# Factorization layer in float32: five wide trees of seven, squared-weight sums on ScalarE's accumulator, one queue for the first loads

## Chip, cores and metric

One core of one Trainium2 chip runs the whole kernel. The metric is the device time of one execution in microseconds; shown are the median and the extremes of three runs. Engine names in the profile: PE is TensorE, PEld its weight loads, DVE is VectorE, ACT is ScalarE, POOL is GpSimd, SP is SyncE (which here only issues loads and stores).

## What is computed

```python
def _L0_rec_ref(x, weight, lin_w, lin_b):      # x (1024, 512), weight (64, 512, 512), lin_w (512, 512)
    out_lin = x @ lin_w.T + lin_b
    xv = jnp.einsum('bf,efm->bem', x, weight)
    zp = jnp.einsum('bf,efm->bem', jnp.square(x), jnp.square(weight))
    interaction = 0.5 * jnp.sum(jnp.square(xv) - zp, axis=1)
    return out_lin + interaction
```

All is float32. The large part is `xv`: 1024 x 512 times 512 x (64 x 512). Its squares are summed over e (64 values). The term `zp` needs no large product: summed over e it is x² times the sum over e of weight², so the kernel builds that sum (512 x 512, tile `w2_sum`) and multiplies once, at the end.

## The kernel before, in words

**Tiling.** The output columns m come in groups: two of 16 and twenty of 24 columns. With e innermost a group of 24 has 24 x 64 = 1536 columns of weight, split into two halves (quadrants `w11`, `w12`, `w21`, `w22` by half of f and half of m; a quadrant is 2 chunks of 128 rows of f, 768 columns each).

**Outer level.** Each group is multiplied by a fast 2 x 2 x 2 scheme of seven products (Winograd's form of Strassen's), products 1 to 7 in the order 1, 6, 5, 2, 7, 4, 3. Their right operands are the four quadrants and the sums `T1`, `T2`, `w12` += `w22`, `w21` += `T2`, which DMAs with accumulation form (issued by POOL). Their left operands are seven sums of x, tiles `X1` to `X7`, prepared once at the start.

**Inner level.** Each outer product is again a fast scheme, a "tree". `tree` is the thin one: 7 products, two row blocks each, right operand 384 columns wide. `wide_tree` is a scheme of 20 products with 256 columns each; it is used for the outer products in `HK` and only in the groups of 24. The sums of weight columns that a tree needs are made on POOL into the ring `t`. Intermediate sums live in PSUM: banks `b1` and `b3` and the pairs `b2_0`, `b2_1` (the profile leaves the numbers out: `b`, with `_l` and `_r` for the two banks of a pair). ACT copies PSUM parts from bank to bank or to SBUF (`p5`, `p53`, shown as `p`), DVE adds finished parts to the targets `oa`, `ob`, `oc`, `od`. For an outer product in `EARLY`, the first parts are added to the earlier target at once on DVE, without a copy kept in `p`. `finish` squares a target (ACT) and sums it over e (DVE, `TENSOR_REDUCE acc<-...`).

**Squared weight.** `w_squares` squares each chunk of a quadrant on ACT into a scratch tile `wsq` and reduces it over e on DVE into `w2_sum`.

**Order.** The program is written as a list of operations with reads, writes and estimated costs. `Plan.order` simulates the engines and puts the operations of each engine into a fixed order by due times; the table `AHEAD_OF` shifts single due times. Additions whose operands are all in SBUF may go to DVE or POOL, whichever comes first in that simulation; those that read PSUM go to DVE. A wait is a semaphore wait in front of an instruction, and every engine works its list in order.

**Start and end.** First x and `lin_w` are loaded and the linear part is multiplied by the same outer scheme (`outer_products`), while the X tiles are prepared. At the end the same function multiplies x² with `w2_sum`, and the parts are joined and stored.

Of the kernel before, what the change touches and what calls it, by code (L numbers as in the profile page):

```python
# [16 lines left out]
P = 128  # L17
SEG = 128
ORDER = (1, 6, 5, 2, 7, 4, 3)
HK = (1, 5, 2, 7)  # L20
EARLY = (2, 7)
# [17 lines left out]
P53S = 2  # L39
AHEAD_OF = """  # L40
0:t6x 1:t29 2:2qu 3:2w 4:3gd7 5:2mat 6:-i 7:t4v 8:1kwd 9:1xp9 a:v6a b:xxr c:-4 d:3jg2 e:-r f:-j g:-r h:-2g
i:-g j:4x k:t l:-8 m:-2k n:1x o:4i6 p:2c q:9 r:-1w s:n t:-11 u:-1 v:-o w:17 x:1n y:1z z:k 10:-23 11:g 12:-16
13:4 14:24 15:r 16:-5 17:z 18:j 19:-k 1a:13 1b:-18 1c:e 1d:-2z 1e:4 1f:21 1h:17 1i:-f 1j:-k 1k:-1 1l:1m 1m:-5
1n:-26 1o:-o 1p:q 1q:-b 1r:1p 1s:-22 1t:9 1u:-10 1v:-5 1w:8 1x:-9 1y:i 1z:1u 20:1e 21:-10 22:o 23:-n 24:-2x
25:2 26:-2t 27:-1z 28:2c 29:1b 2a:1z 2b:-b 2c:22 2d:-23 2e:1p 2f:4 2g:-2y 2h:-j 2i:1h 2j:o 2k:9 2l:k 2m:-c
2n:1i 2o:-1z 2p:-2 2q:47 2r:2n 2s:-6 2t:c 2u:-20 2v:10 2w:-2 2x:-m 2y:-10 2z:i 30:4p 31:5c 32:1j 33:9 34:2x
35:n 36:-6 37:-2c 38:d 39:1e 3a:-n 3b:r 3c:1t 3d:j 3e:m 3f:2k 3g:-2s 3h:1v 3i:31 3j:-12 3k:-m 3l:-2f 3m:7b
3n:2 3o:1co 3p:-i 3q:e 3r:-1h 3s:1nz 3t:-1l 3u:3 3v:118 3w:17 3x:-x 3y:-1t 3z:n 40:r 41:4 42:-v 43:18 44:2pm
45:1j 46:-l 47:-t 48:-1c 49:l3 4a:b 4b:2g 4c:e 4d:36 4e:y 4f:1v 4g:16 4h:-q 4i:b 4j:1 4l:-1r 4m:-3c 4n:n 4o:z
4p:-f 4q:-1d 4r:13 4s:5 4t:y 4u:2g 4v:4 4w:1i 4x:1c 4y:-20 4z:1z 50:l 51:-12 52:-20 53:27 54:-z 55:9 56:-2s  # L50
57:1o5 58:g 59:-1j 5a:-2r 5b:2k 5c:i 5d:21 5e:-12 5f:-1q 5g:1ju 5h:2d 5i:25 5j:p 5k:-1l 5l:-k 5m:-1y 5n:3b
5o:h 5p:-3r 5q:20 5r:-28 5s:-b 5t:2a 5u:29 5v:-n 5w:-2b 5x:w1 5y:3 5z:-1e 60:22 61:-1u 62:24i 63:-1u 64:-33
65:5m 66:-r 67:3q 68:-13 69:11 6a:22 6b:p 6c:s 6d:-y 6e:e 6f:25 6g:k 6h:-o 6i:-1n 6j:1c 6k:-u 6l:u 6m:e8
6n:-2f 6o:-1j 6p:z 6q:1m 6r:23 6s:-x 6t:h 6u:-15 6v:-29 6w:-y 6x:15 6y:-6j 6z:19 70:-n 71:-1n 72:-7 73:1u
74:-1n 75:-2c 76:-1e 77:3p 78:1q 79:7 7a:-2 7b:-u 7c:16 7d:-t 7e:-13 7f:-13 7g:-m 7h:u 7i:-1 7j:1c 7k:2b 7l:1p
7n:r 7o:-d 7p:b 7q:-w 7r:-3a 7s:u 7t:-20 7u:-v 7v:2c 7w:-32 7x:-8c 7y:1a 7z:-5 80:2i 81:-e 82:-2a 83:-2j
84:-29 85:-27 86:-j 87:d 88:-16 89:-2v 8a:-1g 8b:-c 8c:fk 8d:-c 8e:-g 8f:-2d 8g:-k 8h:i 8i:1i 8j:z 8k:-5
8l:-1a 8m:-dh 8n:-a 8o:-d1 8p:a 8q:-k 8r:-f 8s:s 8t:28 8u:q 8v:-19 8w:-1b 8x:3n 8y:-26 8z:fo 90:2s 91:-24 92:b
93:a2 94:-6 95:1h 96:1f 97:2q 98:-2u 99:-39 9a:-1j 9b:-m 9c:-2e 9d:28 9e:-s 9f:yw 9g:-l 9h:-16 9i:-w 9j:a
9k:ln 9l:-j 9m:1 9n:n 9o:1s 9p:-17 9q:r 9r:2p 9s:7 9t:-i 9u:m 9v:41 9w:3h 9x:-2c 9y:-s 9z:-17 a0:7 a1:-t a2:j  # L60
a3:-1x a4:1p a5:5 a6:-a a7:2k a8:-2g a9:14 aa:-u ab:-r ac:-14 ad:7 ae:-r af:-1a ag:-1w ah:-d ai:1vp aj:1a
ak:14 al:-1n am:-v an:w ao:-1b ap:1s aq:u ar:z as:11 at:-11 au:1q av:15 aw:j ax:-1b ay:-2i az:1d b0:-38 b1:-3t
# [12 lines left out]
h1:h h2:27 h4:-1z h5:-2 h6:-h h7:-g h8:-2w h9:-24 ha:1n hb:1c hc:-j hd:3v he:-g hf:-s hg:-1u hh:-3i hi:-n
hj:1a hk:-n hl:-3x hm:-2k hn:-n ho:-24 hp:-31 hq:9 hr:66 hs:-13 ht:4 hu:3t hv:et hw:1c hx:33 hy:33 hz:95
i0:-3c i1:8 i2:1a i3:-t i4:d4 i5:h1 i6:2o i7:-1f i8:-18 i9:i ia:2s ib:-k ic:11 id:-1j ie:-g if:3 ig:-4 ih:q
ii:39 ij:-14 ik:17 il:-2a im:o in:-2z io:29 ip:-1r iq:-11 ir:c is:10 it:-35 iu:-p iv:-1k iw:r ix:-1i iy:-i1
iz:w j0:a j1:b9 j2:-14 j3:1m j4:5d j5:-t j6:-1u j7:-hg j8:-7y j9:-2p ja:2t jb:-ma jc:-69 jd:-qk je:29 jf:-b
jg:3c jh:-2x ji:-4f jj:-9f jk:-2c jl:4d jm:1k jn:-1r jo:-25 jp:li jq:-1z jr:-d jt:4g ju:5o jv:6a jw:-1k jx:3h  # L80
jy:x jz:1q k0:-v k1:-2 k2:z k3:-5k k4:-1z k5:-1l k6:1g k7:8 k8:2g k9:15 ka:-38 kb:-35 kc:-y kd:-u ke:x kf:1u
kg:36 kh:-13 ki:3k kj:3d kk:-c kl:-5b km:vc kn:kz ko:-o kp:11 kq:21z kr:-1a ks:-1c kt:4o ku:ay kv:1p kw:-a3
kx:-y ky:-1d kz:1gq l0:-14 l1:-4h l2:-1a l3:-4 l4:-f l5:2x l6:v l7:-1h l8:t l9:lj la:18x lb:m5 lc:3l ld:-1a
le:-1p lf:4 lg:-2u lh:xt li:20 lj:134 lk:ph ll:-c lm:-1d ln:-1 lo:11 lp:-2n lq:-l lr:di ls:l lt:-p lu:3 lv:14
lw:-19 lx:2i ly:23 lz:-i m0:26 m1:-1h m2:e m3:1l m4:-2w m5:-38 m6:-2 m7:2q m8:-15 m9:-18 ma:-q mb:-1e mc:-11
md:-1v me:-5 mf:19 mg:1y mh:x mi:i mj:-13 mk:28 ml:-ou mm:1f mn:4h mo:-e mp:-9 mq:-q mr:10 ms:-1x mt:e mv:-r
# [263 lines left out]
def kernel(  # L350
# [162 lines left out]
    def lw_in(q, c):  # L513
        o = lw(q, c)
        dma(o.ap, lw_src[:, ts(q * 2 + c, KH * C)], (), o.atoms, 0.65, 2.2, nc.scalar, 0.25)
# [647 lines left out]
```

## Time and profile before

| | |
|---|---|
| median of 3 runs | 1412.26 us (1411.76 to 1416.25) |
| the profiled execution: its own time, its span | 1414.87 us, 1413.1 us |
| mean granted TensorE clock | 0.994 |
| TensorE busy | 1388.7 us, 98% of the span |
| VectorE, ScalarE, GpSimd busy | 1179.7, 825.7, 1173.6 us |
| DMA moved | 251.85 MB, mean 178 GB/s |

The span runs from the first to the last instruction of the profiled execution. A row of the timeline gives the start, the time from the first start to the last end, the instruction, its count and in brackets the idle time of the engine ahead of it with what ended it. A row of the groups gives count, busy time and mean duration in ns of one, then the idle time ahead. A row of the stretches gives the stretch and its length, then busy time and count for PE, PEld, DVE, ACT and POOL, the granted clock, the DMA's busy share and GB/s. A row of the waits gives the total, how often and the longest, in us. A row of the loads gives the count, the KB of one and the median us from issue to landing.

### The profile page before, as it was taken

Reading aid. Unit: us, or ns where it says so; the run is one execution under the profiler, and the core shown is the slowest. Engines: PE = TensorE matmul, PEld = TensorE weight load, DVE = VectorE, ACT = ScalarE, POOL = GpSimd, SP = SyncE. Lnnn points to the kernel's source line nnn. Section 1 sums busy time; section 2 is a strip of 40 time slices with the busy share of each in tenths; the row PEclk is TensorE's granted clock in tenths of the full one; section 3 lists DMA queues with packets and bytes.
Section 4 is the critical chain, followed back from the end, with each engine's and each line's share of the span. In section 5 each row is a group of like instructions: output and inputs, shape, how many; then the busy total and the mean of one; then the engine's idle time right before and its main releaser. Section 6 shows DMA issues by size and latency. Waiting matters only on the chain.

```text
span 1413.1 us, 17921 instructions
## 1 busy us (share of the span) xinstructions
PE 1388.7 (98%) x5500; PEld 1034.9 (73%) x5500; DVE 1179.7 (83%) x1769; ACT 825.7 (58%) x1345; POOL 1173.6 (83%) x1118
## 2 busy tenths in 40 slices
PE   7999999999999999999999999999999999999998
PEld 5878767677776767777776777777677777767666
DVE  5577788888988888888888888888888888898876
ACT  3355555757566565756656565666656565665752
POOL 5999978888788878878887887888788798888884
PEclk8999999999999999999999999999999999999999
DMA  8588595867859596775959577595957759594775
GB/s 248 150 191 195 111 254 126 221 164 178 202 122 243 122 232 154 184 195 127 242 115 247 144 179 199 134 236 116 254 136 183 194 145 228 117 257 117 162 171 131
DMA packets 94943, 251.85 MB, mean 178 GB/s; under 512 B 30464, under 2 KB 33536, under 8 KB 94848
## 3 DMA queue, kind: packets, MB, share of 16 engines
q0 software_dynamic: 27712, 136.23, 49.3%
q1 hardware_dynamic: 66560, 113.43, 23.6%
q10 hardware_dynamic: 576, 1.05, 0.2%
q8 instruction: 45, 0.74, 0.2%
q14 instruction: 50, 0.41, 0.1%
HBM read 127.04 MB, written 6.19 MB: 94 GB/s over the span
## 4 chain that ended last, share of the span: by engine, by line
PE 91%; DMA 4%; POOL 3%; issue 1%; DVE 1%; ACT 0%; SPq 0%; POOLq 0%; ACTq 0%
PE b L490 40%; PE b_r L490 24%; PE b_l L490 24%; POOL t L446 2%; PE b_l L543 2%; PE b_r L543 1%; DMA T<-T1b 1%; DMA oc<-od 1%; DMA T<-T1a 1%; DMA oa<-xT 1%; POOL ob L482 0%; DMA T1a<-weight 0%; DMA w22a<-weight 0%; POOL X L446 0%; DVE oa L446 0%
## 5 line engine op out<-in xcount | busy, mean ns | idle before, releaser
L490 PE MATMUL b<-t,X 128*128 128x384 f32 (+1 forms) x1184 | 401.9, 471 | 3.8 <-DVE ob L446 2.1
L446 POOL TENSOR_TENSOR t<-t,w 128x512 f32<-128x512 f32 (+1 forms) x300 | 293.9, 998 | 36.0 <-PE b L490 25.2
L490 PEld LDWEIGHTS b<-t,X 128*128 128x128 f32 x1184 | 219.2, 190 | 131.2 <-DVE ob L446 10.1
L490 PE MATMUL b_l<-t,X 128*128 128x256 f32 x960 | 243.4, 380 | 0.0
L490 PE MATMUL b_r<-t,X 128*128 128x256 f32 x800 | 214.8, 380 | 0.2 <-POOL t L446 0.2
L490 PEld LDWEIGHTS b_l<-t,X 128*128 128x128 f32 x960 | 180.7, 190 | 34.1 <-ACT b_l L456 2.5
L446 POOL TENSOR_TENSOR t<-w 128x768 f32<-128x768 f32 (+1 forms) x88 | 160.2, 1824 | 33.2 <-DMA w<-T 21.2
L490 PEld LDWEIGHTS b_r<-t,X 128*128 128x128 f32 x800 | 150.3, 190 | 46.0 <-issue 2.8
L463 ACT ACTIVATE oa<-oa 128x768 f32<-128x768 f32 (+1 forms) x176 | 142.7, 823 | 58.6 <-DVE oa L446 47.7
L473 DVE TENSOR_REDUCE acc<-oa 128x12 f32<-128x768 f32 (+1 forms) x176 | 159.2, 921 | 6.8 <-ACT oa L463 6.6
L473 DVE TENSOR_REDUCE w_sum<-wsq 128x12 f32<-128x768 f32 (+1 forms) x176 | 159.1, 919 | 1.4 <-ACT wsq L463 1.2
L490 PE MATMUL b_r<-w,X 128*128 128x256 f32 x600 | 149.7, 380 | 0.5 <-issue 0.5
L490 PEld LDWEIGHTS b_r<-w,X 128*128 128x128 f32 x600 | 112.8, 190 | 20.2 <-ACT b_r L455 1.9
L463 ACT ACTIVATE wsq<-w 128x768 f32<-128x768 f32 (+1 forms) x132 | 107.0, 819 | 32.6 <-DMA w<-weight 22.1
L490 PE MATMUL b_l<-w,X 128*128 128x256 f32 x480 | 117.5, 381 | 0.9 <-ACT b_l L456 0.9
L490 PE MATMUL b<-w,X 128*128 128x384 f32 (+1 forms) x336 | 110.2, 456 | 2.1 <-DMA w<-T 2.1
L456 ACT COPY b<-b 128x768 f32<-128x768 f32 (+1 forms) x74 | 55.4, 748 | 92.0 <-PE b L490 56.8
L490 PEld LDWEIGHTS b_l<-w,X 128*128 128x128 f32 x480 | 90.3, 190 | 17.1 <-ACT b_l L456 4.7
L463 ACT ACTIVATE ob<-ob 128x768 f32<-128x768 f32 (+1 forms) x88 | 72.0, 822 | 47.4 <-DVE ob L446 45.3
L490 PE MATMUL b<-T,X 128*128 128x384 f32 (+1 forms) x264 | 90.3, 477 | 2.2 <-DMA T<-T1a 1.4
L490 PEld LDWEIGHTS b<-w,X 128*128 128x128 f32 x336 | 63.5, 190 | 30.7 <-DMA w<-T 2.5
L473 DVE TENSOR_REDUCE acc<-oc 128x12 f32<-128x768 f32 (+1 forms) x88 | 79.8, 920 | 5.0 <-ACT oc L463 4.8
(179 smaller groups left out, 2620.1 us busy)
## 6 DMA issues: line engine op xcount, KB each, us to landing
w<-weight SPq DMA_DIRECT2D x120, 384.0 KB, 6.9
ob<-od POOLq DMA_DIRECT2D x40, 768.0 KB, 11.4
oc<-od POOLq DMA_DIRECT2D x40, 768.0 KB, 12.9
T<-weight SPq DMA_DIRECT2D x40, 384.0 KB, 5.8
w<-T POOLq DMA_DIRECT2D x20, 768.0 KB, 5.8
T1a<-weight SPq DMA_DIRECT2D x20, 384.0 KB, 3.3
T1a<-weight POOLq DMA_DIRECT2D x10, 768.0 KB, 8.4
w22a<-weight SPq DMA_DIRECT2D x20, 384.0 KB, 10.9
```

Source lines behind the costliest of these rows:

```text
L446: return f(o.ap, a.ap, b.ap)
L456: return nc.scalar.copy(o.ap, i.ap)
L463: lambda _: nc.scalar.activation(o.ap, i.ap, AF.Square, scale=scale),
L473: nc.vector.tensor_reduce(o, x, axis=AX.X, op=ALU.add)
L490: nc.tensor.matmul(a.ap, b.ap, w.ap, start=start, stop=True, skip_group_check=True)
L543: nc.tensor.matmul(a.ap, b.ap, w(k).ap, start=first and k == 0 and j % 2 == 0, stop=True, skip_group_check=True)
```

## The change

Outer product 6 joins `HK`, so that five of seven trees are wide in the groups of 24. Products 3, 4 and 6 join `EARLY`. `w_squares` no longer reduces on DVE: every run of 64 columns (one m, all e) is one ACT instruction that squares into a scratch tile `unread` and writes the sum of its squares through ACT's accumulator into `w2_sum`; the `wsq` tiles go, and there are 2048 such instructions. The first loads of x and `lin_w` are ranked in one fixed order on SP (before, `lin_w` went through ACT's queue). The preparation sums of five X tiles are bound to DVE, one `p53` tile goes, a few costs of the planner are changed, and the table `AHEAD_OF` is another one throughout, so that the order on every engine changes.

```diff
-HK = (1, 5, 2, 7)
-EARLY = (2, 7)
+HK = (1, 5, 6, 2, 7)
+EARLY = (2, 3, 4, 6, 7)
-P53S = 2
+P53S = 1
+SUMMED = ('w11', 'w12', 'w21', 'w22')
+DIRECT = ()
+PREP = (6, 5, 2, 7, 4)
 AHEAD_OF = """
-0:t6x 1:t29 2:2qu 3:2w 4:3gd7 5:2mat 6:-i 7:t4v 8:1kwd 9:1xp9 a:v6a b:xxr c:-4 d:3jg2 e:-r f:-j g:-r h:-2g
...
-            o.latest = latest - ahead[o.sign]
+            o.latest = latest - ahead[o.sign] if o.rank is None else o.rank - 1e6
...
-    wsq_ring = ring([make(f"wsq{k}", WIDE) for k in range(2)])
+    wsq_ring = ring([make(f"wsq{k}", WIDE) for k in range(2 if len(SUMMED) < 4 else 0)])
+    unread = make("unread", E)
...
+    firsts = iter(range(100))
+
+    def first_load(o, i):
+        n = next(firsts)
+        dma(o.ap, i, (), o.atoms, 1.1 if n < 4 else 0.65, 2.2, 0.45, n)
+
     def lw_in(q, c):
-        o = lw(q, c)
-        dma(o.ap, lw_src[:, ts(q * 2 + c, KH * C)], (), o.atoms, 0.65, 2.2, nc.scalar, 0.25)
+        first_load(lw(q, c), lw_src[:, ts(q * 2 + c, KH * C)])
...
+    x_load(0, 0, 0)
     lw_in(0, 0)
-    x_load(0, 0)
+    x_load(0, 0, 1)
+    x_load(0, 1, 0)
     lw_in(1, 0)
-    x_load(0, 1)
+    x_load(0, 1, 1)
     lw_in(0, 1)
     lw_in(1, 1)
-    x_load(1, 1)
-    x_load(1, 0)
-    dma(bias.ap, lin_b.partition_broadcast(P), (), bias.atoms, 1.3, 2.2)
+    for h, q in ((1, 1), (1, 0)):
+        for k in range(KH):
+            x_load(h, q, k)
+    first_load(bias, lin_b.partition_broadcast(P))
...
-            tt(o, a, b, sub)
+            tt(o, a, b, sub, DVE if i in PREP else None)
...
         for k in range(KH):
-            i, sq = reg(w(g, q), k * mi * E, mi * E), reg(wsq_ring(), 0, mi * E)
-            square(sq, i)
+            i = reg(w(g, q), k * mi * E, mi * E)
             o = reg("w2_sum", (row * KH + k) * M + base[g] + col * mi, mi)
-            reduce(o.ap, sq, o.atoms)
+            if q not in SUMMED:
...
+            for m in range(0, mi, 4):
+
+                def emit(_, i=i, o=o, m=m):
+                    return [
+                        nc.scalar.activation(
+                            reg(unread).ap, Reg(i.tile, i.off + j * E, E).ap,
+                            AF.Square, accum_out=Reg(o.tile, o.off + j, 1).ap,
+                        )
+                        for j in range(m, m + 4)
+                    ][-1]
+
+                plan.add({ACT: 4 * 0.18}, emit, Reg(i.tile, i.off + m * E, 4 * E).atoms,
+                         Reg(o.tile, o.off + m, 4).atoms + reg(unread).atoms)
...
-        dma(four(r), lin_dram[:, c, ts(h, 4), :], (("lin", h, c),), r.atoms)
+        dma(four(r), lin_dram[:, c, ts(h, 4), :], (("lin", h, c),), r.atoms, 2.3)
...
-        dma_add(four(r, 0, cut), acc_dram[:, c, ts(h, 4), :cut], 4 * C,
+        dma_add(four(r, 0, cut), acc_dram[:, c, ts(h, 4), :cut], 5 * C,
```

How the order moves, at three places. In the rows a tile carries a number (`X_62` to `X_68` are X1 to X7, `w_69` is `w11`, `w_70` is `w12`, `w_71` is `w21`, `T_76` is `T2`), and what an instruction waits for stands in brackets: `Activation` is ACT's own signal, `DMAHW` and `DMASW` are loads.

First place: ACT in a group of the steady part, around the squares of `w12` and `w11` between the thin trees 4 and 3 and the next group's tree 1. Before:

```order
L463 ACTIVATE wsq_86<-w_70 128x768 [waits DMAHW4_49,DMASW3_49,DVE_49]
L463 ACTIVATE oa<-oa 128x2x384 [waits DVE_49] x2
L456 COPY p_1_83<-b 128x768 [waits PE_49]
L456 COPY b_1<-b 128x2x384 [waits PE_49]
L463 ACTIVATE oa<-oa 128x2x384 [waits Pool_49]
L463 ACTIVATE wsq_87<-w_70 128x768 [waits DMAHW5_49,DVE_49]
```

With the change, from one PSUM copy (`b_0<-b`) to the next (`b_1_l<-b_r`):

```order
L459 COPY b_0<-b 128x2x384 [waits PE_49]
L755 ACTIVATE unread,w_sum<-w_69 128x64 [waits Activation_49] x4
L466 ACTIVATE oa<-oa 128x2x384 [waits DVE_49]
L755 ACTIVATE unread,w_sum<-w_69 128x64 [waits DMAHW3_49,Activation_49]
L755 ACTIVATE unread,w_sum<-w_69 128x64 [waits Activation_49] x11
L755 ACTIVATE unread,w_sum<-w_71 128x64 [waits DMAHW3_49,DMASW5_49,Activation_49]
L755 ACTIVATE unread,w_sum<-w_71 128x64 [waits Activation_49] x3
L466 ACTIVATE oa<-oa 128x2x384 [waits DVE_49]
L466 ACTIVATE ob<-ob 128x2x384 [waits DMASW7_49,DVE_49]
L755 ACTIVATE unread,w_sum<-w_71 128x64 [waits Activation_49] x4
L459 COPY b_1_l<-b_r 128x512 [waits DVE_49,PE_49]
```

One square of a whole chunk, which waited for DVE to free a `wsq` tile, is now a run of single pieces, each of which waits for ACT's own signal; in all 32 pieces and 3 squares of `oa` and `ob` stand between these two copies (rows that repeat are left out above).

Second place: SP at the start. Before:

```order
L478 DMA oa<-xT 128x512 x2
L478 DMA ob<-xT 128x512 x2
L478 DMA oa<-xT 128x512 x4
L478 DMA od<-lin_b 128x512
L478 DMA w_69<-weight 128x512 x2
```

With the change:

```order
L481 DMA oa<-xT 128x512
L481 DMA ob<-lin_wT 128x512
L481 DMA oa<-xT 128x512 x2
L481 DMA ob<-lin_wT 128x512
L481 DMA oa<-xT 128x512
L481 DMA ob<-lin_wT 128x512 x2
L481 DMA ob<-xT 128x512 x2
L481 DMA oa<-xT 128x512 x2
L481 DMA od<-lin_b 128x512
L481 DMA w_69<-weight 128x512
```

All first loads stand on SP in the order in which the linear part uses them, ahead of the first weights.

Third place: PE in the thin trees 4 (`X_65`) and 3 (`X_64`) of a steady group. In tree 4 `b<-t` is product 5, in tree 3 too; product 3 writes to the same bank. Before:

```order
L490 MATMUL b<-t,X_65 128x384 x2
L490 MATMUL b_0_r<-t,X_68 128x256
L490 MATMUL b_1<-t,X_65 128x384 x2
L490 MATMUL b<-w_71,X_65 128x384 x4
L490 MATMUL b<-t,X_64 128x384 x2
L490 MATMUL b<-w22a,X_64 128x384 x4
```

With the change:

```order
L494 MATMUL b<-t,X_65 128x384 x2
L494 MATMUL b_0_r<-t,X_68 128x256
L494 MATMUL b_1<-t,X_65 128x384 x2
L494 MATMUL b<-w_71,X_65 128x384 x4
L494 MATMUL b<-t,X_64 128x384 x2
L494 MATMUL b<-w22a,X_64 128x384 x2
L494 MATMUL b_1<-t,X_65 128x384 x2
```

In tree 4 the same matmuls lie between products 5 and 3. In tree 3 the old order ran product 1 and product 3 right behind product 5, the new one has a product of tree 4 between them.

234 lines of the change are left out of this document (121 added, 113 removed).

## The prediction

> **What bounds the kernel now.** I read the page's busy times first, then the chain that ended last, then the busy times by stretch, then what TensorE waited for.
>
> ```profile
> PE 1388.7 (98%) x5500; PEld 1034.9 (73%) x5500; DVE 1179.7 (83%) x1769; ACT 825.7 (58%) x1345; POOL 1173.6 (83%) x1118
> PE 91%; DMA 4%; POOL 3%; issue 1%; DVE 1%; ACT 0%; SPq 0%; POOLq 0%; ACTq 0%
> 0.00:20.00 20.00, 10.80 (x26) 7.20 (x27) 6.50 (x8) 5.75 (x7) 8.07 (x12) 0.74 0.88 299
> 615.48:739.90 124.42, 124.20 (x490) 91.68 (x489) 107.81 (x162) 76.45 (x124) 104.33 (x97) 1.00 0.74 180
> PE b_l L543 <- DMA oa<-xT: 7.6, 1, 7.6
> ```
>
> TensorE is busy for 98% of the span and is 91% of the chain. The stretch 615.48 to 739.90 is two groups of 24 columns in the steady part: TensorE has work in 124.20 of 124.42 us, at a granted clock of 1.00. There the other engines have room: per group of 62.2 us, DVE works 53.9, ACT 38.2, POOL 52.2. Only the first 20 us show a long wait, 7.6 us for the first x. So the time is the sum of the matmuls; what shortens them counts in full as long as no other engine passes 61 us per group.
>
> **The change part by part.** *1. Tree 6 becomes wide in the 20 groups of 24 columns.* A thin tree is 7 products of 2 halves of 384 columns, a wide one is 20 products of 256; every float32 matmul stands in the trace as two instructions.
>
> ```profile
> 628.34 1.45 PE L490 MATMUL b<-t,X 128*128 128x384 f32 x4
> 629.63 1.45 PE L490 MATMUL b<-w22b,X 128*128 128x384 f32 x4
> 656.61 1.89 PE L490 MATMUL b_l<-T1a,X 128*128 128x256 f32 x8
> 658.33 1.89 PE L490 MATMUL b_r<-T1a,X 128*128 128x256 f32 x8
> ```
>
> From start to start, 4 instructions of 384 columns take 1.29 us (0.3225 each) and 8 of 256 take 1.72 (0.215 each). Thin: 28 x 0.3225 = 9.03. Wide: 40 x 0.215 = 8.60. That saves 0.43 per group, 20 x 0.43 = **8.6 us**. The same prices give 61.5 us for a group before (84 and 160 instructions) and 61.1 after (56 and 200); the 0.7 us between 61.5 and the measured 62.2 are small gaps that I leave as they are.
>
> *2. POOL and DVE.* POOL now makes tree 6's wide sums (one of 768, two of 512, four of 256) in place of one of 768 and two of 384. In return the wider EARLY set puts tree 6's, 3's and 4's first addend into the target straight from PSUM on DVE, so that three adds per group leave POOL.
>
> ```profile
> L446 POOL TENSOR_TENSOR t<-t,w 128x512 f32<-128x512 f32 x120 | 158.7, 1325 | 22.3 <-PE b L490 16.5 <-PE b_l L490 0.7
> L446 POOL TENSOR_TENSOR t<-t,w 128x256 f32<-128x256 f32 x180 | 135.6, 780 | 13.7 <-PE b L490 8.7
> L446 POOL TENSOR_TENSOR t<-T,t 128x384 f32<-128x384 f32 x40 | 40.0, 1001 | 3.1
> L446 POOL TENSOR_TENSOR ob<-p,ob 128x768 f32<-128x768 f32 x20 | 37.7, 1885 | 0.0
> L446 POOL TENSOR_TENSOR oa<-oa,oc 128x768 f32<-128x768 f32 x20 | 37.4, 1870 | 8.7 <-ACT oa L463 8.2 <-issue 0.5
> L446 POOL TENSOR_TENSOR ob<-ob,oa 128x768 f32<-128x768 f32 x20 | 36.3, 1816 | 3.8 <-ACT b_l L456 3.8
> L473 DVE TENSOR_REDUCE w_sum<-wsq 128x12 f32<-128x768 f32 x160 | 148.7, 944 | 0.5 <-ACT wsq L463 0.5
> L446 DVE TENSOR_TENSOR ob<-b,oa 128x768 f32<-128x768 f32 x60 | 57.3, 955 | 5.5 <-PE b L490 4.3 <-issue 0.5
> L446 DVE TENSOR_TENSOR oc<-ob,b_l 128x512 f32<-128x512 f32 x60 | 40.3, 683 | 3.4 <-ACT b_r L456 2.3 <-PE b_l L490 0.4
> L446 DVE TENSOR_TENSOR oc<-ob,b_r 128x256 f32<-128x256 f32 x120 | 46.6, 416 | 4.9 <-ACT p L456 3.8 <-PE b_r L490 0.3
> ```
>
> POOL per group: the 768 sum is in both; + 2 x 1.325 + 4 x 0.780 - 2 x 1.001 = +3.8, and three adds leave, -5.6: 50.4 of 61.1. DVE per group: eight reductions leave (148.7 / 20 = -7.4), three adds of 768 leave (-2.9), ten adds of 256 and five of 512 come (+4.2, +3.4): 51.2. Both get lighter, so neither costs time. One wait moves: in the thin trees 4 and 3 product 3 now overwrites the bank of product 5 after a DVE add (0.955) instead of an ACT copy (0.798, row below). The order of TensorE puts 1.7 us (tree 4) and 2.6 us (tree 3) of other matmuls between the two products; that covers it. Uncovered it would be 0.16 x 40 = 6 us.
>
> *3. ACT.* Off ACT: eight squares of 768, three copies p and one copy b of 768 per group. Onto it: tree 6's wide copies (four of 512, one of 256), and 96 squares of 64 columns per group whose sum goes out through the accumulator.
>
> ```profile
> L463 ACT ACTIVATE wsq<-w 128x768 f32<-128x768 f32 x120 | 99.6, 838 | 18.9 <-DMA w<-weight 16.8 <-DVE oa L446 1.3 <-DVE w_sum L473 0.2
> L456 ACT COPY p<-b 128x768 f32<-128x768 f32 x60 | 47.9, 798 | 22.4 <-PE b L490 21.1
> L456 ACT COPY b<-b 128x768 f32<-128x768 f32 x60 | 47.4, 790 | 80.7 <-PE b L490 46.1 <-DVE oc L446 32.4 <-PE b_r L490 1.0
> L455 ACT ACTIVATE b_r<-b_r 128x512 f32<-128x512 f32 x80 | 46.8, 585 | 30.0 <-DVE b_r L446 29.2
> L456 ACT COPY p<-b_r 128x256 f32<-128x256 f32 x120 | 44.8, 373 | 41.3 <-PE b_r L490 33.9 <-PE b_l L490 5.6 <-DVE oa L446 1.2
> L455 ACT ACTIVATE X<-X 128x128 f32<-128x128 f32 x4 | 1.2, 306 | 0.4 <-POOL X L446 0.4
> L456 ACT COPY t<-t 128x4 f32<-128x4 f32 x1 | 0.2, 195 | 0.0
> 706.65 0.59 ACT L455 ACTIVATE oa<-b_l 128x512 f32<-128x512 f32 x1
> 707.13 0.38 ACT L455 ACTIVATE oa<-b_r 128x256 f32<-128x256 f32 x1
> ```
>
> Without the pieces ACT has 38.2 - 8 x 0.83 - 3 x 0.80 - 0.79 + 4 x 0.58 + 0.37 = 31.1 us per group. The price c of a piece has no row. The rows of 128 and 768 columns differ by 0.83 ns a column, so a row of 64 lasts about 0.25. Independent instructions overlap: the row of 0.59 at 706.65 is followed after 0.48, so a free piece could start every 0.14 us. That is the lower end. But every piece writes the same scrap tile `unread`, and the order shows that each waits for ACT's own signal, so no piece begins before the last one has ended. What such a wait on the own engine costs, DVE shows:
>
> ```profile
> 583.62 0.94 DVE L473 TENSOR_REDUCE w_sum<-wsq 128x12 f32<-128x768 f32 x1
> 584.48 0.94 DVE L473 TENSOR_REDUCE acc<-oc 128x12 f32<-128x768 f32 x1
> 586.73 0.96 DVE L446 TENSOR_TENSOR ob<-b,oa 128x768 f32<-128x768 f32 x1
> 587.72 0.95 DVE L446 TENSOR_TENSOR ob<-ob,b 128x768 f32<-128x768 f32 x1
> ```
>
> A free instruction follows 0.08 before the end of the row ahead of it, the chained one (it adds to what was just written) 0.03 after. A chained piece is then 0.25 + 0.03 = 0.28 us if the sum costs nothing more, and if writing it out is a small step of its own (the copy of 4 columns, 0.195) 0.475: the upper end. I take 0.28, the row that a piece is most like. ACT has then 31.1 + 96 x 0.28 = 58.0 of 61.1 us, under TensorE but at 95%. ACT works in order, so a PSUM copy behind a run of pieces is late, and TensorE waits for copies (`b<-b`, `b_l<-b_l`): I charge 0.1 us per group, **+2 us**, between 0 and what rivals A and B give.
>
> The Trainium skill, ScalarE: Activation LUTs, section What ACT_TABLE_LOAD costs, gives an ACTIVATE with immediates 186 ns + 0.833 ns a column, with an overlap of about 93 ns between neighbours. For 64 columns this is 0.24 in a chain and 0.15 without; the 306 ns row is 13 ns above it, so the trace nearly agrees, and by 0.24 ACT would have 54 us per group.
>
> *4. First loads.* TensorE's first real matmul starts late:
>
> ```profile
> oa<-xT SPq DMA_DIRECT2D x6, 256.0 KB, 4.6
> L446 POOL TENSOR_TENSOR X<-X 128x256 f32<-128x256 f32 x48 | 43.2, 949 | 18.8 <-ACT X L456 6.0 <-DVE X L446 5.5 <-PE b_r L543 4.6
> 0.74 0.87 SPq L478 DMA_DIRECT2D oa<-xT  x2
> 5.21 1.04 ACT L456 COPY X<-oa 128x1024 f32<-128x1024 f32 x1 [2.98 <-DMA oa<-xT]
> 12.62 3.78 PE L543 MATMUL b_l<-ob,oa 128*128 128x256 f32 x8 [7.61 <-DMA oa<-xT]
> ```
>
> SP issues one load each 0.43 us; the first pair was issued by 1.61 and used by ACT at 5.21, 3.6 us later. Now the two loads of the first matmul, and the x behind them, are the first three on SP: issued by 2.04, landed about 5.7 instead of 12.6. The gain is at most 6.9 us. The loads behind them take 256 KB / 299 GB/s = 0.88 us each whatever their order, and the weights still come after all 13, so part is lost again where the first groups wait for DMA and POOL. Below it is 0. I take **5 us**: the operands of every later product of this stage land before TensorE gets to it. That tree preparation of five X moves from POOL to DVE takes 0.95 us each off a POOL that the first groups wait for; I count nothing for it.
>
> Sum: -8.6 - 5 + 2 = -11.6. It is made against the profiled execution (span 1413.1, its own time 1414.87, 2.6 above the median of 1412.26) and carried over to the median: **1401 us**.
>
> **The rivals.**
> A. ACT becomes the bound, slower. The place is the chain of pieces, the point a price of 0.324 us: then 31.1 + 96 c is the 62.2 us of a group before. If the written-out sum is an instruction of its own that overlaps by the 0.11 of the 706.65 row, c = 0.25 + 0.03 + 0.195 - 0.11 = 0.365 and a group takes 66.1: 1412 - 5 + 20 x 3.9 = 1485. At 0.475 it is 76.7, 1697. For it: the self-wait, and that no row shows a sum for free; against it: no row of ACT shows a separate step either. The Trainium skill, VectorE: DVE Perf Modes, section Two Vector instructions with no wait between them, says that an operation of VectorE that writes out its accumulator is two instructions; for ACT no run here shows it. This rule speaks for A.
> B. ACT stays below TensorE, but the runs are too long. In one group of the new order ACT has 32 pieces and 3 squares of `oa` and `ob` between two PSUM copies; at 0.28 these are 9.0 + 2.5 = 11.5 us, and 3 us less at a price of 0.19, the row of the smallest copy. If a third of these 3 us reaches TensorE, 1 us per group: 1401 - 2 + 20 = 1419. For it: 95% of ACT; against it: DVE at 87% of a group lets TensorE run now.
> C. The change of the loads does nothing. TensorE starts earlier and waits later, in the groups of 16, for DMA and POOL: 1406. For it: DMA is busy for 0.88 of the first 20 us.
>
> **How the numbers follow.** The forecast (1391 to 1407) has 0.42, C 0.14, B 0.14, A 0.30. A measurement of this kernel tells 0.3% (4 us) from no change. Faster takes the forecast and C, 0.56; B lies about the upper edge of no change, 0.08 there and 0.06 above it; with A slower has 0.36. The likeliest case's own range is 1391 to 1407. Half of A, where the written-out sum overlaps, lies under 1490; above that 0.15 and below 1391 some 0.03 are left out: 1391 to 1490.
>
> **What would show it.** Step 1: 200 matmul instructions of 256 columns per group instead of 160, 56 of 384 instead of 84, and a pair of groups at 123 to 124 us; over 126 would tell against it. Step 3: the rows of `unread,w_sum`; starts 0.28 apart confirm the price, above 0.32 is rival A, and then the chain of waits has ACT in it and TensorE waits for `b_l<-b_l`. Step 2: no TensorE wait for DVE at bank b in trees 3 and 4. Step 4: the first real matmul at about 6 us, and the first tree's start 5 us earlier. The forecast is wrong if ACT's busy time per pair of groups passes 122 us.

## The result, and the profile after

The changed kernel takes **1672.67 us** (median of 4 runs, 1671.54 to 1673.64) against 1413.49 us (4 runs) for the kernel before: **1.1831 times as long, 95% interval 1.1808 to 1.1854**, 259 us more. The forecast was 1401, and the range ended at 1490.

The page of the changed kernel: busy times, the chain by engine, and the two rows of the pieces on the tiles `w` of three quadrants (the fourth, in `w22a` and `w22b`, has 256 more of each tile).

```profile
PE 1457.3 (87%) x5740; PEld 1087.6 (65%) x5740; DVE 1131.4 (68%) x1860; ACT 1325.4 (79%) x5280; POOL 1116.9 (67%) x1124
ACT 57%; PE 35%; issue 5%; DMA 2%; POOL 1%; DVE 0%; SPq 0%; ACTq 0%; DVEq 0%; POOLq 0%
L755 ACT ACTIVATE unread<-w 128x64 f32<-128x64 f32 x1536 | 392.5, 256 | 55.9 <-DMA w<-weight 13.7
L755 ACT ACTIVATION_READ_ACCUMULATOR unread<-w 128x1 f32 x1536 | 287.1, 187 | 0.0
```

The bound has moved. Before, TensorE was 91% of the chain; now it is 35%, and ACT is 57%. And each piece is two rows: the square (256 ns) and a read of the accumulator (187 ns), which the program does not show as an instruction.

One stretch of 1000 us in the steady part, for the kernel before and then for the changed one (columns as in the stretches above: PE, PEld, DVE, ACT, POOL, clock, DMA share, GB/s):

```profile
240.00:1240.00 1000.00, 999.78 (x3927) 736.80 (x3926) 869.00 (x1308) 612.57 (x996) 838.97 (x772) 1.00 0.74 180
```

```profile
240.00:1240.00 1000.00, 873.86 (x3427) 648.06 (x3426) 681.48 (x1137) 818.42 (x3265) 666.73 (x652) 0.98 0.62 147
```

A group has 244 matmul instructions before and 256 now. Per group that is 244 / 3927 x 1000 = 62.1 us before and 256 / 3427 x 1000 = 74.7 us after. Nothing is at its limit in the second row: TensorE has work for 87% of the time and ACT for 82%. Each waits for the other in turn.

The timeline of ACT shows a run of pieces in the changed kernel:

```profile
800.24 0.26 ACT L755 ACTIVATE unread<-w 128x64 f32<-128x64 f32 x1
800.40 0.18 ACT L755 ACTIVATION_READ_ACCUMULATOR unread<-w 128x1 f32 x1
800.62 0.26 ACT L755 ACTIVATE unread<-w 128x64 f32<-128x64 f32 x1
```

The read begins 0.16 us after its square; the next square begins 0.22 after the read, 0.04 behind the read's end. A piece every **0.38 us**, where the prediction had 0.28.

What a run does to TensorE: pieces and one square of `ob`, the last piece at 821.45, stand on ACT ahead of the copy `b_l<-b_r`. The timeline of ACT, then of TensorE, and the stretches around them, all of the changed kernel:

```profile
821.45 0.26 ACT L755 ACTIVATE unread<-w 128x64 f32<-128x64 f32 x1
821.61 0.19 ACT L755 ACTIVATION_READ_ACCUMULATOR unread<-w 128x1 f32 x1
821.71 0.58 ACT L459 COPY b_l<-b_r 128x512 f32<-128x512 f32 x1
```

```profile
822.43 1.19 PE L494 MATMUL b_r<-t,X 128*128 128x256 f32 x2 [3.95 <-ACT b_l L459]
```

```profile
820.00:824.00 4.00, 1.57 (x4) 1.33 (x5) 0.92 (x2) 3.91 (x14) 0.35 (x1) 0.56 1.06 222
824.00:828.00 4.00, 4.00 (x13) 3.21 (x12) 1.76 (x4) 3.50 (x7) 0.89 (x1) 0.58 0.56 114
828.00:832.00 4.00, 4.00 (x20) 3.54 (x19) 3.42 (x7) 3.81 (x19) 2.56 (x3) 1.00 0.18 29
```

TensorE stands still for 3.95 us, and then works at a granted clock of 0.56 to 0.58 until 828: 13 matmul instructions in 4 us instead of 20. An estimate from these rows: 7 instructions are missing there and some 3 between 822.43 and 824, at 0.215 us each, so a wait of this length costs some 2 us more than itself. (The Trainium skill, TensorE: Matmul & The Clock Gate, section What's actually happening, puts the clock at half after an idle window of about 3.4 us; the trace agrees.) The two largest of TensorE's waits for ACT (total, times, longest):

```profile
PE b_r L494 <- ACT b_l L459: 68.8, 27, 4.1
PE b L494 <- ACT b L459: 36.5, 21, 3.4
```

TensorE's idle time rose from 1413.1 - 1388.7 = 24 us to 1669.8 - 1457.3 = 213 us, its busy time by 69 us although it has less to multiply: 188 + 69 = 257 of the 259.

### The profile page after: what moved, and what is told of

It is laid out like the page before. It is cut to its first block, busy times and chain, and to the rows that moved or that the text cites. A ratio compares the mean times of both kernels' runs of the same rounds, so it can differ in the third digit from the quotient of the medians.

```text
span 1669.8 us, 22301 instructions
## 1 busy us (share of the span) xinstructions
PE 1457.3 (87%) x5740; PEld 1087.6 (65%) x5740; DVE 1131.4 (68%) x1860; ACT 1325.4 (79%) x5280; POOL 1116.9 (67%) x1124
## 4 chain that ended last, share of the span: by engine, by line
ACT 57%; PE 35%; issue 5%; DMA 2%; POOL 1%; DVE 0%; SPq 0%; ACTq 0%; DVEq 0%; POOLq 0%
ACT unread L755 37%; PE b_l L494 14%; PE b_r L494 14%; PE b L494 5%; ACT b_l L459 3%; ACT oa L466 3%; ACT oc L466 3%; ACT p L459 2%; ACT ob L466 2%; ACT b L459 1%; ACT b_r L458 1%; ACT b_r L459 1%; ACT oa L458 1%; DMA w<-weight 1%; PE b_r L553 1%
## 5 line engine op out<-in xcount | busy, mean ns | idle before, releaser
L755 ACT ACTIVATE unread<-w 128x64 f32<-128x64 f32 x1536 | 392.5, 256 | 55.9 <-DMA w<-weight 13.7
L494 PE MATMUL b_r<-t,X 128*128 128x256 f32 x1000 | 289.1, 402 | 97.9 <-ACT b_l L459 68.8
L449 POOL TENSOR_TENSOR t<-t,w 128x512 f32<-128x512 f32 x300 | 310.6, 1064 | 37.9 <-PE b L494 28.6
L494 PE MATMUL b<-t,X 128*128 128x384 f32 (+1 forms) x864 | 290.3, 467 | 45.4 <-ACT b L459 36.5
L494 PE MATMUL b_l<-t,X 128*128 128x256 f32 x1200 | 314.8, 389 | 1.4 <-ACT b_l L459 0.4
L755 ACT ACTIVATION_READ_ACCUMULATOR unread<-w 128x1 f32 x1536 | 287.1, 187 | 0.0
L476 DVE TENSOR_REDUCE acc<-ob 128x12 f32<-128x768 f32 (+1 forms) x88 | 80.5, 923 | 44.3 <-ACT ob L466 44.3
L449 POOL TENSOR_TENSOR t<-t,T 128x256 f32<-128x256 f32 (+1 forms) x100 | 93.9, 951 | 21.2 <-PE b_l L494 15.9
L449 DVE TENSOR_TENSOR oa<-b,oc 128x768 f32<-128x768 f32 (+1 forms) x88 | 81.9, 931 | 33.0 <-PE b L494 30.4
L449 POOL TENSOR_TENSOR t<-t 128x256 f32<-128x256 f32 x100 | 74.1, 741 | 34.0 <-PE b L494 33.6
```

The costliest lines, as they stand in the source:

```text
L449: return f(o.ap, a.ap, b.ap)
L476: nc.vector.tensor_reduce(o, x, axis=AX.X, op=ALU.add)
L494: nc.tensor.matmul(a.ap, b.ap, w.ap, start=start, stop=True, skip_group_check=True)
L755: nc.scalar.activation(reg(unread).ap, Reg(i.tile, i.off + j * E, E).ap, AF.Square, accum_out=Reg(o.tile, o.off + j, 1).ap,)
```

## The experiments

The two theories of the first expectations: theory 1, the self-wait on the one scratch tile `unread`, which puts every piece behind the end of the last one; theory 2, the new order of the trees and adds is slow by itself. Beside them, a third suspect: the runs stand at places that suit the planner's price of 0.18 us and not the real one. In the table, "same order" means that every instruction that is left stands where the change puts it; "planned anew" means that the planner laid the order out again, with the price that the row gives and, where it says so, with pieces for fewer quadrants. `AHEAD_OF` was the same in all of these.

| kernel | one piece every | us | to before, interval |
|---|---|---|---|
| the change | 0.38 | 1672.67 | 1.1831 (1.1808 to 1.1854) |
| same order, no pieces | none | 1408.46 | 0.9972 (0.9953 to 0.9990) |
| same order, four scratch tiles | 0.24 | 1457.31 | 1.0314 (1.0297 to 1.0330) |
| same order, one tile, no sum written | 0.288 | 1500.22 | 1.0618 (1.0597 to 1.0639) |
| same order, sums on DVE | none | 1444.39 | 1.0218 (1.0202 to 1.0233) |
| one tile, planned anew at 0.38 | 0.38 | 1584.98 | 1.1211 (1.1188 to 1.1234) |
| four tiles, planned anew at 0.24 | 0.24 | 1414.89 | 1.0009 (0.9998 to 1.0020) |
| four tiles, two quadrants, planned anew at 0.24 | 0.24 | **1408.53** | **0.9967 (0.9955 to 0.9979)** |
| one tile, two quadrants, planned anew at 0.38 | 0.38 | 1432.12 | 1.0144 (1.0128 to 1.0160) |
| sums on DVE, planned anew | none | 1451.91 | 1.0281 (1.0261 to 1.0301) |
| before, pieces in four tiles | 0.24 | 1586.69 | 1.1222 (1.1207 to 1.1238) |
| before, new first loads | | 1412.54 | 0.9998 (0.9989 to 1.0007) |
| four tiles, same order, old first loads | 0.24 | 1458.22 | 1.0316 (1.0302 to 1.0330) |

### Four scratch tiles in turn

```diff
+    scrap = ring([unread] + [make(f"scrap{k}", E) for k in range(3)])
...
-                            reg(unread).ap, Reg(i.tile, i.off + j * E, E).ap,
+                            reg(scrap()).ap, Reg(i.tile, i.off + j * E, E).ap,
```

> The changed kernel with four scrap tiles in turn instead of the one tile unread; the order on every engine is the same, only the wait of each piece on the one just ahead of it goes. Theory 1 (the pieces are dear because each waits for the end of the last one's accumulator read, 0.38 us from start to start): the pitch falls to 0.25 (0.16 from the square to the read, 0.09 from a read to an unchained next row, both as the changed kernel's timeline has them), ACT has 31 + 96 x 0.25 = 55 us per group, under TensorE's 61, and the time is 1395 to 1425. Theory 2 (the new order itself, with five wide trees, one p53 tile and the early adds, makes TensorE wait, whatever a piece costs): above 1550.

It took 1457.31 us. The timeline of ACT in this kernel:

```profile
802.59 0.28 ACT L756 ACTIVATE unread<-w22a 128x64 f32<-128x64 f32 x1
802.74 0.22 ACT L756 ACTIVATION_READ_ACCUMULATOR unread<-w22a 128x1 f32 x1
802.83 0.27 ACT L756 ACTIVATE scrap<-w22a 128x64 f32<-128x64 f32 x1
```

The read stays, but the next square begins 0.09 after the read's start instead of 0.22: 0.24 us per piece. 2048 pieces x 0.14 = 287 us less on ACT gave 215 us back. The time lies in neither of the two ranges: theory 1 holds for most of the loss, but 44 us over the kernel before remain.

### No pieces at all

```diff
-                def emit(_, i=i, o=o, m=m):
...
+                emit = None
```

> The changed kernel without its 2048 pieces (the sums of the squared weight are left at zero, so that work is left out); the order of all else is the same. Theory 1: ACT has 31 us per group and TensorE is the bound again: 1413 - 8.6 - 5 to 7 = 1398 to 1400, a pair of groups at 123 to 124 us. Theory 2: above 1450, with TensorE waits for copies or DVE.

1408.46 us (10 runs, 1401.98 to 1415.04): a little faster than before, so theory 2 falls. The order of trees and adds is not slow, and what the pieces cost in it is 1672.7 - 1408.5 = 264 us. It also bounds what the rest of the change brings: terms 1 and 4 alone make 1413.1 - 8.6 - 5 = 1399.5, so some 9 us are missing; they are looked for under the prediction's steps. (This kernel sets `w2_sum` to zero before its first matmul, which comes at 7.10 us instead of 5.25 in the next kernel; but the first tree starts at 31.27 against 31.41, so that this doesn't explain them.)

### The sums on DVE, in the places of the pieces

```diff
+                    if m == 0:
+                        return nc.scalar.activation(sq.ap, i.ap, AF.Square)
+                    if m == 4:
+                        return nc.vector.tensor_reduce(
...
```

> The changed kernel with the sums of the squared weight made as before (a square of a whole chunk on ACT into two wsq tiles, the sum over e on DVE), put out at the places where the order has the first and the second run of pieces of a chunk. Theory 1: ACT 37 us per group, DVE 51 + 7.4 = 58.6 of 61: TensorE stays the bound or nearly, 1400 to 1420. If DVE at 96% stalls TensorE, 1420 to 1460. Theory 2: above 1500.

A whole chunk is squared where its first run of pieces stood and reduced where its second stood. 1444.39 us. DVE was busy for 87% and TensorE waited for its `ob` (12.4 us) and `oa` (8.3 us). The order leaves no room on DVE for the reductions; below, the planner was given the chance to make it.

### The price of 0.38 given to the planner

```diff
-                plan.add({ACT: 4 * 0.18}, emit, Reg(i.tile, i.off + m * E, 4 * E).atoms,
+                plan.add({ACT: 4 * 0.38}, emit, Reg(i.tile, i.off + m * E, 4 * E).atoms,
```

> The changed kernel with the planner's cost of a piece at 0.38 us, as measured, instead of 0.18; the pieces stay chained, the planner only places them otherwise. If the time is ACT's sum (31.1 + 96 x 0.38 = 67.6 us per group, 5.4 more than a group before), it goes to about 1515. If it stays near 1670, the places of the runs don't matter and something else than ACT's sum sets the pace; between the two, the difference is what the planner's wrong price cost on top of the sum.

1584.98 us: the places are worth 88 of the 264 us. What is left is near what rival A's sum gives at 0.38 (31.1 + 96 x 0.38 = 67.6 us per group, 1412 - 5 + 20 x 5.4 = 1515) and 70 us above it, so even a planner that knows the price doesn't get ACT to work without gaps. In this kernel DVE and then TensorE wait like this:

```profile
DVE ob L449 <- DMA ob<-od: 51.0, 24, 3.8
PE b L494 <- DVE ob L449: 32.6, 28, 4.2
```

The add that needs a target still being filled by a DMA comes up again under step 2.

### The piece that the prediction assumed

```diff
-                            AF.Square, accum_out=Reg(o.tile, o.off + j, 1).ap,
+                            AF.Square,
```

> The changed kernel in its own order, with the one scratch tile, but the pieces don't write a sum out: the squares are made and nothing is kept, the sums of the squared weight are left out (set to zero at the start). This is the piece that the prediction assumed: chained, with the sum for free. If its price for the chain is right, a piece begins 0.28 us after the last one, and ScalarE has 31.1 + 96 x 0.28 = 58.0 of 61.1 us per group. The forecast then said 1401, rival B 1419. If, as the four tiles at 0.24 us (1457) suggest, ScalarE's queue in this order is late long before its sum reaches TensorE's, the time is 1465 to 1520. If the pitch is 0.24 or less, the time is 1457 or less.

The timeline of ACT, the 1000 us of the steady part, and two of TensorE's waits for ACT (the largest in all, and the longest single one) in this kernel:

```profile
799.86 2.27 ACT L759 ACTIVATE unread<-w 128x64 f32<-128x64 f32 x8
240.00:1240.00 1000.00, 951.84 (x3827) 709.28 (x3827) 765.01 (x1270) 791.93 (x2261) 750.97 (x734) 1.00 0.69 167
PE b_r L494 <- ACT b_l L459: 23.3, 18, 1.8
PE b L494 <- ACT p L459: 1.9, 1, 1.9
```

Eight pieces in 2.27 us, the last one 0.256 long: one every (2.27 - 0.256) / 7 = 0.288 us. The price for a chained square, 0.28, was right to 3%. But the kernel took **1500.22** us, not 1401, and not rival B's 1419: ACT has 31.1 + 96 x 0.288 = 58.7 us of work per group, and a group takes 256 / 3827 x 1000 = 66.9. So the forecast would have failed by 99 us even if the sum had been free; the read of the accumulator brought the other 172. Of these, 41 are TensorE's busy time (1457.3 against 1416.4 us), at a mean granted clock of 0.976 against 0.998.

Four kernels now have the same order and differ only in what a piece holds ACT for. Against no pieces, 0.24 us adds 2048 x 0.24 = 492 us of work to ACT and 49 us to the time (a tenth); from 0.24 to 0.288, 98 more on ACT and 43 in the time (44%); from 0.288 to 0.38, 188 more on ACT and 172 in the time (92%). (The two without sums start their first matmul some 2 us later, for the zeros.) A share arrives long before ACT's sum reaches TensorE's 61.1 us, which it does at a price of 0.31, and it grows. The last step crosses that price, so it holds the overflow of rival A as well; how much of it each brings can't be told apart here.

### Four tiles, and the price of 0.24 given to the planner

The two edits above together, with `4 * 0.24`.

> The changed kernel with four scratch tiles in turn, and the planner's price of a piece raised from 0.18 to the 0.24 us that the four tiles showed, so that the runs of pieces stand at other places. If the 49 us that the four tiles still cost against no pieces at all (1457 against 1408) are runs put at places for which the price was too low, the time falls to 1405 to 1430. If they are the work itself (every PSUM copy queues behind some run, wherever it stands), it stays at 1440 or more.

1414.89 us: of the 49 us that the four tiles cost over no pieces, 42 were placing. With both the self-wait and the wrong price gone, five wide trees with all sums on ACT are as fast as the kernel before, no faster.

### The kernel before, with pieces

```diff
-            square(sq, i)
-            reduce(o.ap, sq, o.atoms)
+            def emit(_, i=i, o=o):
+                for j in range(mi):
+                    nc.scalar.activation(
+                        reg(scrap()).ap, Reg(i.tile, i.off + j * E, E).ap,
...
+            plan.add({ACT: 0.10 + 0.00083 * sq.size}, emit, i.atoms, sq.atoms)
+            plan.add({DVE: 0.08 + 1.06 * sq.size / 1024}, None, sq.atoms, o.atoms)
```

> The kernel before, with every square of a chunk replaced by 12 (or 8) pieces of 64 columns into four scratch tiles in turn, and without VectorE's reduction; the order is the old one. ScalarE then has 38.2 - 6.6 + 96 x 0.24 = 54.6 us per group of 62.2, VectorE 46.5. If only the sum of ScalarE's work counts, the time is 1400 to 1416. If a run of pieces (2.9 us in place of 0.84) makes the PSUM copies behind it late, it is 1425 to 1460 with TensorE waiting for ScalarE's copies.

Busy times, the first wait of TensorE, and the 1000 us of the steady part:

```profile
PE 1429.5 (90%) x5500; PEld 1036.0 (65%) x5500; DVE 1035.7 (65%) x1593; ACT 1163.2 (73%) x5265; POOL 1173.5 (74%) x1118
PE b_r L491 <- ACT b_l L457: 45.0, 28, 3.3
240.00:1240.00 1000.00, 908.57 (x3466) 650.36 (x3465) 667.49 (x1038) 764.43 (x3479) 739.68 (x683) 0.99 0.65 157
```

ACT is busy for 73% of the span, DVE is relieved of 144 us, no piece waits for itself, and it is 174 us slower, far beyond both expected ranges. Runs of 12 pieces (12 x 0.24 = 2.9 us) stand where a square of 0.84 stood, and the copies behind them are late. This is rival B by itself, in another order. (The planner had the old price here too; planned anew it was not tried.)

### Fewer pieces: two quadrants, with four tiles and with one

```diff
-SUMMED = ('w11', 'w12', 'w21', 'w22')
+SUMMED = ('w12', 'w21')
```

with `4 * 0.24` and four tiles, and then with `4 * 0.38` and the one tile.

> The changed kernel with pieces for two quadrants alone (w12, w21), in four scratch tiles in turn at a price of 0.24 us; the other two are squared in chunks and reduced by VectorE. Per group ScalarE has 31.1 + 4 x 0.83 + 48 x 0.24 = 45.9 us, VectorE 51.2 + 3.7 = 54.9, both well under TensorE's 61.1. If what remains above 1400 with all four quadrants on the four tiles (1414.9) is ScalarE's queue, the time falls to 1400 to 1408 and is below both kernels; if it is something else in the new order (the added waits on VectorE, say), it stays at 1411 to 1418.

> As the one with pieces for two quadrants in four scratch tiles, but with the one scratch tile of the change and a planner's price of 0.38 us. ScalarE has 31.1 + 3.3 + 48 x 0.38 = 52.7 us per group, less than the 54.1 of four quadrants on four tiles. If only ScalarE's sum counts, the time is at most 1415. If the length of a run counts (4 chained pieces hold the queue 1.5 us instead of 1.0), it is 1420 or more.

With four tiles **1408.53 us**, faster than the kernel before by 4 us, 0.3%; the interval does not reach 1. With one tile 1432.12, although ACT's sum (52.7 us per group) is below that of four quadrants on four tiles (54.1), which took 1414.89. So the sum alone doesn't decide. The length of a run may be the reason; but the two kernels also differ in the order and in DVE's work (54.9 against 51.2 us per group), so that this is not shown. The 1000 us of the steady part with two quadrants on four tiles:

```profile
240.00:1240.00 1000.00, 993.88 (x4109) 772.72 (x4108) 867.24 (x1429) 727.52 (x2505) 805.73 (x788) 1.00 0.74 180
```

256 / 4109 x 1000 = 62.3 us per group, no less than the 62.1 before. So the 4 us are not won in the steady part. This kernel's first tree starts at 31.23 us, the one of the kernel before at 40.60.

### Five wide trees with the old sums, planned anew

`SUMMED = ()` in place of the line above.

> The changed kernel without the pieces: all four quadrants are squared by ScalarE in chunks and reduced by VectorE as before, and the planner lays out the order for that. The five wide trees and the new first loads stay. If the wide trees are worth what term 1 says and VectorE has room, the time is 1402 to 1408. VectorE, though, has 51.2 + 7.4 = 58.6 of 61.1 us per group then; if it cannot carry the reductions beside the three adds that came to it, the time is 1420 to 1444 (1444 is what the same work cost when it was only put at the pieces' places), with TensorE waiting for VectorE.

1451.91 us, above the range and also above the 1444.39 of the same work at the pieces' places. From the page and the waits of this kernel:

```profile
PE 1397.7 (96%) x5740; PEld 1072.5 (74%) x5740; DVE 1258.6 (87%) x2036; ACT 800.6 (55%) x1360; POOL 1115.7 (77%) x1124
PE b L495 <- DVE ob L450: 20.2, 21, 5.2
```

So in no order tried here could DVE carry the reductions beside the adds that come with the wide tree, and the sums on ACT are its relief: half of them (1408.5) is better than all (1414.9) and than none (1451.9). `AHEAD_OF` belongs to the change as it was, so the last two may have been held back by it; that was not tried.

### The first loads

In the kernel before, with the new order of the 13 loads on SP and all else in its place:

```diff
+    NEW = (1, 0, 2, 4, 3, 5, 6, 7, 8, 9, 10, 11, 12)
...
+                for k in NEW:
+                    nc.sync.dma_start(*loads[k])
```

> The kernel before, with one thing changed: its 13 first loads go out on SyncE's queue in the order of the change; every other instruction keeps its place. If term 4 of the prediction is right, TensorE's first real matmul moves from 12.6 to about 5.5 us, the rest of the program follows as before and the time falls by 5 to 7 us, to 1406 to 1408. If rival C is right (TensorE starts earlier and waits later for loads or GpSimd), the first matmul is as early, but the time stays at 1411 to 1414.

1412.54 us, no difference. The timeline of TensorE and then of ACT in this kernel:

```profile
5.32 3.01 PE L556 MATMUL b_l<-ob,oa 128*128 128x256 f32 x8
14.65 3.48 PE L556 MATMUL b_l<-ob,oa 128*128 128x256 f32 x8 [4.59 <-ACT b_l L456]
40.38 1.03 PE L490 MATMUL b<-t,X 128*128 128x256 f32 x4
```

```profile
9.42 1.04 ACT L456 COPY X<-oa 128x1024 f32<-128x1024 f32 x1 [7.19 <-DMA oa<-xT]
14.02 0.58 ACT L456 COPY b_l<-b_l 128x512 f32<-128x512 f32 x1
```

The first real matmul starts at 5.32 instead of 12.62, as forecast. The first tree starts at 40.38 instead of

```profile
40.60 1.03 PE L490 MATMUL b<-t,X 128*128 128x256 f32 x4
```

(this row is the kernel before). ACT has three copies of x in its list ahead of `b_l<-b_l` (the first is shown); the x that the first one needs now comes after others, so it starts at 9.42 instead of 5.21, and TensorE waits 4.59 us for `b_l`. 7.3 us were won, and 7.1 given back before the first tree: 4.6 at this wait, 9 us later, and most of the rest at two shorter ones behind it (1.55 us for `T1b`, 1.28 for `b_l`).

The other way about, the change with four tiles and the old loads:

```diff
+    OLD = [(k, nc.sync) for k in (3, 5, 9, 8, 11, 10)] + [(1, nc.scalar), (7, nc.scalar)]
+    OLD += [(0, nc.sync), (4, nc.scalar), (2, nc.sync), (6, nc.scalar), (12, nc.sync)]
```

> The changed kernel with four scratch tiles in turn (1457 us as run) and the old order and queues of the first loads; all else keeps its place. If the loads are worth what term 4 says, the time rises by 5 to 7 us, to 1462 to 1464; if the changed kernel's first groups give the earlier start back, it stays at 1456 to 1458.

1458.22 against 1457.31 us: no difference either. TensorE with the old loads, and then with the new ones: the first tree and the first group of 24.

```profile
38.06 1.03 PE L495 MATMUL b<-t,X 128*128 128x256 f32 x4
130.89 0.70 PE L495 MATMUL b_r<-t,X 128*128 128x256 f32 x2 [0.78 <-DVE ob L450]
```

```profile
32.37 1.03 PE L495 MATMUL b<-t,X 128*128 128x256 f32 x4
128.75 0.70 PE L495 MATMUL b_r<-t,X 128*128 128x256 f32 x2 [0.78 <-DVE ob L450]
```

Here ACT's list fits the loads: 5.7 us are still there at the first tree, 2.1 at the first group of 24, and none at the end. In the order that is fastest (two quadrants) the old loads were not tried, so what they are worth there is open.

## Why the prediction was wrong

**Step 3 failed, in its price and in what follows from the price.** The price c was bounded by 0.14 and 0.475, and 0.28 was chosen, the price of a chained piece "if the sum costs nothing more". The chain was right (0.288 measured without the sum). The sum was not free: it is a row of its own, 187 ns, of which 0.09 us count in a chain (0.38 - 0.288). Rival A had this instruction at 0.365; its chance of 0.30 was the largest beside the forecast's. (The rule of the Trainium skill, VectorE: DVE Perf Modes, section Two Vector instructions with no wait between them, an operation that writes out its accumulator is two instructions, is stated for VectorE. The rows of `ACTIVATION_READ_ACCUMULATOR` show the same on ScalarE.)

The second part is the term for late copies. The prediction saw the mechanism ("a PSUM copy behind a run of pieces is late, and TensorE waits for copies"), but ACT's sum was "under TensorE but at 95%", and so it charged 0.1 us per group, 2 us in all. At nearly the price that it used, 0.288, the kernel took 1500.2, 92 us more than without pieces: 4.6 per group. The premise behind it stands at the head of the prediction: what shortens the matmuls "counts in full as long as no other engine passes 61 us per group". It doesn't hold here: no engine passed it in that kernel. Rival A too goes by the sum alone ("the point a price of 0.324 us"); the change took 1673 where A's own sum gives 1515 at 0.38. ACT works its list in order, the PSUM copies that free TensorE's banks stand in the same list, and the planner had placed the runs for 0.18. Rival B named this place and this mechanism ("32 pieces and 3 squares of `oa` and `ob` between two PSUM copies"), and sized it at 18 us, from a guess that a third of the delay of one run per group arrives. It was 1500.2 - 1408.5 = 92 us, and at 0.38 the time is above A's sum as well: A and B were not alternatives.

**Step 1, the fifth wide tree (outer product 6).** The price of a matmul was right, but of the 8.6 us only about half arrived, and in the steady part hardly any. TensorE's rows at the first wide product of the first group of 24, at a product with `T1a` that comes in every second group, at the same product 14 groups later, and at the last thin product of the last group are these, of the kernel before and then of the one without pieces:

```profile
132.12 0.59 PE L490 MATMUL b_r<-t,X 128*128 128x256 f32 x2
282.36 0.59 PE L490 MATMUL b_r<-T1a,X 128*128 128x256 f32 x2
1152.72 0.59 PE L490 MATMUL b_r<-T1a,X 128*128 128x256 f32 x2
1384.01 1.45 PE L490 MATMUL b<-t,X 128*128 128x384 f32 x4
```

```profile
128.45 0.70 PE L494 MATMUL b_r<-t,X 128*128 128x256 f32 x2 [0.78 <-DVE ob L449]
277.71 0.59 PE L494 MATMUL b_r<-T1a,X 128*128 128x256 f32 x2
1147.44 0.59 PE L494 MATMUL b_r<-T1a,X 128*128 128x256 f32 x2
1375.96 1.45 PE L494 MATMUL b<-t,X 128*128 128x384 f32 x4
```

From end to end 1251.9 against 1247.5 us: 4.4 saved, and 4.2 missing. But the 14 steady groups took 870.36 against 869.73: 0.6 saved of 14 x 0.43 = 6.0. A pair of groups takes 124.2 us there, where the prediction had 123 to 124. The rest of the 4.4 was won in the groups ahead of these and behind them. (And the two profiled executions lie 8.7 us apart, the medians 4.7, so the 4.4 is the favourable end.)

**Step 2 failed in a part that was declared free.** Its sums of work were right: without pieces, per group of 62.1 us, ACT works 31.0 us (predicted 31.1), DVE 50.8 (51.2) and POOL 50.1 (50.4). The row is the 1000 us of the steady part of that kernel:

```profile
240.00:1240.00 1000.00, 995.11 (x4117) 774.97 (x4116) 818.32 (x1367) 498.39 (x882) 806.85 (x789) 1.00 0.74 180
```

What was wrong is the wait. Step 2 compared a DVE add of 0.955 us with an ACT copy of 0.798 at the same place and found 1.7 us of cover. It overlooked what else the add needs. The copy `p<-b` needed only the bank. The add `ob<-b,ob` also needs its target, and the target is being filled by the DMA `ob<-od`. The waits of DVE for that DMA, in the kernel before and in the one without pieces, with TensorE's wait that follows:

```profile
DVE ob L446 <- DMA ob<-od: 0.4, 1, 0.4
```

```profile
DVE ob L449 <- DMA ob<-od: 24.5, 24, 2.2
PE b L494 <- DVE ob L449: 6.1, 11, 1.8
```

The bank stays full until the DMA has landed and the add is done, and TensorE waits 6.1 us for that add in the whole kernel, 2.9 of them in the 14 steady groups, where 5.4 are missing. In the kernel before there is no such wait in those groups. So it is a cause of the missing time; that it is the cause of all of it was not shown. The prediction's "Uncovered it would be 0.16 x 40 = 6 us" had the size by another cause, which is luck. Leaving 3 and 4 out of `EARLY` would separate the two; it was not tried.

**Step 4, the first loads.** The first matmul came at 5.37 us in the changed kernel (forecast: about 6), but in both kernels on which the loads alone were changed they made no difference: there rival C was right. C looked for the loss in the groups of 16, at DMA and POOL. In the kernel before it sat already in front of the first tree, in ACT's list. In the changed kernel itself the pieces took it:

```profile
27.32 0.26 ACT L755 ACTIVATE unread<-w 128x64 f32<-128x64 f32 x1
27.57 0.58 ACT L459 COPY b_l<-b_l 128x512 f32<-128x512 f32 x1
```

```profile
28.21 3.43 PE L553 MATMUL b_l<-w22b,X 128*128 128x256 f32 x8 [3.85 <-ACT b_l L459]
36.91 1.03 PE L494 MATMUL b<-t,X 128*128 128x256 f32 x4
137.14 0.70 PE L494 MATMUL b_r<-t,X 128*128 128x256 f32 x2 [0.78 <-DVE ob L449]
```

24 pieces in a row (from 18.57 on) stand ahead of `b_l<-b_l`. The first tree is 3.7 us early, and the first group of 24 (132.12 before) is 5 us late. Without pieces the first tree starts at 31.27, 9.3 us early, and that group at 128.45, 3.7 early: so 5.6 are lost in the groups of 16, the place that C named, though there TensorE waits mostly for DVE and ACT. The 3.7 last to the end; how much of it the loads bring, and how much the X tiles prepared on DVE, was not separated.

**What stays open.** Why one tile, planned anew at 0.38, is still 70 us above ACT's own sum was seen only in part, in the two waits shown with that run. Whether it is the length of the runs or something else in the order that makes a share of ACT's work arrive below its limit was not tested by itself: no run kept the work and changed only the length of the runs.

## What to carry to other kernels

An engine that works in order is not safe because its sum is below the bound (here 58.7 of 61.1 us of work cost 92 us): compare the longest run of work in front of each instruction for which another engine waits, with the time that this other engine can go on without it. When a scheduler places the work, its price for a new instruction has to come from a measured row first; with 0.18 for 0.38 a third of the loss (88 of 264 us) was placing alone. When an operation takes the place of another one, list all its operands: the add was slower by 0.16 us and late by a DMA.

## What the runs showed of the hardware

Writing out the accumulator on ScalarE is a second instruction: 187 ns for a row, 0.09 us of the pitch where the squares are chained (0.38 against 0.288). Where they are not, the read begins 0.15 us behind its square and the next square 0.09 behind the read. A wait for the engine's own last instruction, through a scratch tile that nobody reads, cost 0.14 us per piece, as much as half a square; four tiles in turn removed it. And a wait of TensorE of nearly 4 us was followed by some 5 us at a little over half the clock; in the kernel at 0.288, where no wait for ACT is longer than 1.9 us, the mean granted clock was 0.998, against 0.976 in the changed kernel.
